# Expert-choice routing in a fused attention and MoE kernel: the chosen tokens by place and gather instead of a product over all tokens

## The chip, the cores and the metric

The kernel runs on one core of a Trainium2 chip. The metric is the device time of one execution in microseconds (us), the median of several runs. Names of engines: PE is TensorE (matmul), PEld its weight load, DVE VectorE, ACT ScalarE, POOL GpSimd, SP SyncE, which here issues nearly all DMAs. All data is fp32.

## The reference, cut to what matters

The input is four images x[B=4, C=128, 64, 64]; S = 4096 places of an image are its tokens. Layer 0 is group norm, three 1x1 convolutions with PReLU, and a softmax attention over all places with 64-wide queries and keys. Layer 1 is, on tokens, a layer norm with an attention of width 128, then a layer norm with a mixture of 64 experts in which each expert chooses tokens:

```python
logits = einsum('bsd,ed->bse', x, gate_w) + gate_b
probs = softmax(logits, axis=1)                      # over the tokens
vals, idx = top_k(probs.transpose(0, 2, 1), 8)       # 8 tokens per expert
gathered = take_along_axis(x, idx)                   # [b, 8, 64, 128]
pooled = einsum('bked,bke->bed', gathered, topv)
h = gelu([pooled, 1] @ weight1[e])                   # 128(+1) -> 512
out = [h, 1] @ weight2[e]                            # 512(+1) -> 128
outputs = zeros; outputs.at[idx].add(out * topv)     # scatter-add, then residual
```

## The kernel before, in words

The work is cut into 8 query blocks of 512 tokens per image and layer; a block goes through 8 groups of four 128-key chunks. A step of the main loop is one group: scores on PE (L526), exp on ACT (L535), and one step later the product with the values on PE (L460 for layer 0, L488 for layer 1). In layer 0 DVE sums the exps (L547, L550); in layer 1 DVE forms sums and differences of the values' and exps' halves (L474 to L476, the "mix") for a product with fewer multiplications.

Eight attentions follow each other as `stage(image, layer, beside, ...)`: (0,0), (1,0), (0,1), (2,0), (1,1), (3,0), (2,1), (3,1). In each step a stage advances, by one item, a generator `beside` (norms, convolutions, keys, routing), one for the next block's queries, and the finishing work of the block before, `after`; a barrier of the scheduler ends the step, so the order of each engine's instructions is nearly that of the program. The engines work their own queues in order and wait for each other by semaphores; buffers come from pools by tag, and a new tile in a tag waits for the last reader of what lay there.

The finish of a layer-1 block (`finish_attn`) norms the tokens (L174 is the norm's power, on POOL; L175 to L178 and L333 on DVE), stores the normed tokens `tb` to DRAM (L627 or L639), and leaves logits in M (a pair of images shares a tile, experts of one on each 64 partitions) with the eight largest of each 512 as candidates (L665). The last block's residual tokens in channels are `xp`, stored by L630.

The routing of image b, `route(b, take)`, goes: the eight largest logits of each expert (L689); a copy z of the logits in which these eight are replaced by a large negative value (L692, match_replace over 64x4096); exp of M with its sum (L700); exp of z (L710); the difference M = exp(M) - exp(z), which holds the eight weights at their places and zeros elsewhere (L711; on POOL for b = 0 to 2, on DVE for b = 3). Then the tokens are loaded (L678, eight of 256 KB), M is transposed by 32 PE transposes (L737, copied by ACT at L740), and 64 matmuls (as the profile counts them; L729) give the pooled tokens of the experts in two halves, which are scaled by the inverse sums (`inv2`, L718 to L722; L747) and added by a small matmul against `twin` (L750, L751). M stays for the scatter at the end: a product of the experts' outputs with M.

Routing 0 runs beside the stage (2,0), routing 1 beside (3,0), routing 2 beside (3,1), and routing 3 in the tail after all attention. The tail: `w1b` and seven token blocks are loaded, then weights 2 to 5 into a ring of four buffers (weights 0 and 1 are there already); the last block is finished; routing 3; weights 6, 7, 8 into buffers named k, z and v, 9 to 15 through the ring (L830, L834; 2.1 MB for each group of four experts). The FFN runs over 16 groups: first product (L912, `ph`), transposes (L922), GELU, second product (L942, `po`). Then the y tiles are read back (L976), the scatter product (L989) is added to them (L994) and they are stored from ACT's queue (L996).

The kernel takes its exps without subtracting a maximum. A guard therefore checks sums and inverses (L1466 to L1480, thirteen small DVE instructions), adds the verdicts over the partitions with a matmul (L1486, `pc`), reads the `count` (L1487) and branches: if a check fails, a general version runs, which with these inputs it doesn't.

Of the kernel before, what the change touches and what calls it, by code (L numbers as in the profile page):

```python
# [9 lines left out]
F32 = mybir.dt.float32  # L10
AF = mybir.ActivationFunctionType
ALU = mybir.AluOpType
# [14 lines left out]
def tile_unshifted(  # L27
# [48 lines left out]
    def ms_tile(name):  # L76
        return ps_ms.tile([P, BLK], F32, tag="ms", name=name)

    def block_tile(tag, name, bufs=2):
        pool = pools[of_pool.get(tag, "blk")]  # L80
        return pool.tile([P, BLK], F32, tag=tag, name=name, bufs=bufs)

    def dram_tile(shape, name):
        return dram.tile(shape, F32, tag=name, name=name)
# [5 lines left out]
    t1 = [[dram_tile([P, BLK], f"t1_{b}_{n}") for n in range(NB)] for b in range(B)]  # L90
    t2 = [[dram_tile([P, BLK], f"t2_{b}_{n}") for n in range(NB)] for b in range(B)]
    x1T = [[dram_tile([P, SUB, C], f"xT_{b}_{n}") for n in range(NB)] for b in range(B)]
    tokens = [[dram_tile([P, SUB, C], f"tk_{b}_{n}") for n in range(NB)] for b in range(B)]
    first_pair = dram_tile([P, S], "first_pair")

    e1 = [[dram_tile([CR, BLK], f"e1_{b}_{n}") for n in range(NB)] for b in range(B)]
# [463 lines left out]
    def finish_conv(b, n):  # L560
# [18 lines left out]
        yield  # L579
        turn_to_tokens(xp, block_tile("tb", f"xt{nm}"), x1T[b][n])  # L580

    def finish_attn(b, n):
        nm = f"{b}_1_{n}"
        av = avs.pop((b, 1, n))
# [39 lines left out]
        tg = block_tile("c1", f"tg{nm}")  # L624
        if b == B - 1 and n == NB - 1:
            norm_tokens(xT, tb, f"l2_{b}_{n}")
            nc.sync.dma_start(out=tokens[b][n], in_=tb)  # L627
            xp = block_tile("xp", f"xp{nm}")
            to_channels(xT, xp, f"x2_{b}_{n}")
            nc.sync.dma_start(out=x2[b][n], in_=xp)  # L630
            yield
            to_channels(tb, tg, f"l2_{b}_{n}")
        else:
            turn_to_channels(
                xT.rearrange("p s c -> p (s c)"), block_tile("xp", f"xt{nm}"), x2[b][n]
            )
            yield
            norm_tokens(xT, tb, f"l2_{b}_{n}")
            nc.sync.dma_start(out=tokens[b][n], in_=tb)  # L639
            turn_to_channels(  # L640
                tb.rearrange("p s c -> p (s c)"), block_tile("c0", f"tt{nm}"), t2[b][n]
            )
            yield
            yield
            nc.sync.dma_start(out=tg, in_=t2[b][n])
            yield
# [22 lines left out]
    pooled = keep.tile([P, E, B], F32, tag="pooled", name="pooled")  # L669


    twin = const.tile([P, 2, E], F32, tag="twin", name="twin")
    for h in range(2):
        nc.gpsimd.tensor_add(twin[:, h, :], ident[:, :E], ident[:, E:])
    inv_tot = keep.tile([P, B // 2], F32, tag="inv_tot", name="inv_tot")

    def load_tokens(b, tok, n):
        nc.sync.dma_start(out=tok[:, bass.ts(n, SUB), :], in_=tokens[b][n])  # L678

    def route(b, take):  # L680

        hs = slice((b % 2) * E, (b % 2 + 1) * E)
        m = M[b // 2][hs, :]
        neg = small.tile([P, 1], F32, tag="r_neg", name=f"r_neg{b}")
        tot = small.tile([P, 4], F32, tag="r_tot", name=f"r_tot{b}")
        top = small.tile([P, 8], F32, tag="r_top", name=f"r_top{b}")
        nc.vector.max(out=top[hs, :], in_=cand[b][hs].rearrange("p n k -> p (n k)"))  # L689
        nc.vector.tensor_scalar(neg[hs, :], top[hs, 0:1], -1.0, None, op0=ALU.mult)  # L690
        z = take("z")[hs, :]
        nc.vector.match_replace(  # L692
            out=z, in_to_replace=top[hs, :], in_values=m, imm_value=-3.0e38
        )
        yield
        own = take("e")
        ex = m if own is None else own[hs, :]
        quarter = [bass.ts(i, S // 4) for i in range(4)]
        for i, part in enumerate(quarter):
            nc.scalar.activation(  # L700
                ex[:, part], m[:, part], AF.Exp, bias=neg[hs, :], accum_out=tot[hs, i : i + 1]
            )
            if i % 2 == 1:
                yield
        inv = inv_tot[hs, b // 2 : b // 2 + 1]
        nc.vector.tensor_reduce(tot[hs, 0:1], tot[hs, :], axis=AX.X, op=ALU.add)
        nc.vector.reciprocal(inv, tot[hs, 0:1])
        subtract = nc.vector.tensor_sub if b == B - 1 else nc.gpsimd.tensor_sub
        for i, part in enumerate(quarter):
            nc.scalar.activation(z[:, part], z[:, part], AF.Exp, bias=neg[hs, :])  # L710
            subtract(m[:, part], ex[:, part], z[:, part])  # L711
            if i % 2 == 1:
                yield
        tok = take("tok")
        for n in range(NB - 1 if b == B - 1 else 0, NB):
            load_tokens(b, tok, n)
        p2 = ms_tile(f"inv2_{b}")
        nc.tensor.matmul(  # L718
            p2[:, 0:1], lhsT=twin[hs].rearrange("p h e -> p (h e)"), rhs=inv, start=True, stop=True
        )  # L720
        inv2 = small.tile([P, 1], F32, tag="r_inv2", name=f"inv2_{b}")
        nc.vector.tensor_copy(inv2, p2[:, 0:1])  # L722
        mT = take("mT")
        per = BLK // E

        def pool_tokens(pp, js):

            for j in js:
                nc.tensor.matmul(  # L729
                    pp[bass.ts(j % 2, E), :C], lhsT=mT[:, j, :], rhs=tok[:, j, :],  # L730
                    start=(j < 2), stop=(j >= NJ - 2),
                )

        for g in range(NJ // per):
            pm = ms_tile(f"pmt{b}_{g}")
            for s in range(per):
                nc.tensor.transpose(  # L737
                    pm[:, bass.ts(s, E)], m[:, bass.ts(g * per + s, P)], ident[hs, hs]
                )
            nc.scalar.copy(mT[:, bass.ts(g, per), :], pm.rearrange("p (s e) -> p s e", e=E))  # L740
            yield
        pp = ms_tile(f"pp{b}")
        pool_tokens(pp, range(NJ))
        if b == 1:
            nc.sync.dma_start(out=first_pair, in_=M[0])
        halves = take("halves")[:, :C]
        nc.vector.tensor_scalar(halves, pp[:, :C], inv2, None, op0=ALU.mult)  # L747
        yield
        pq = ms_tile(f"pool{b}")
        nc.tensor.matmul(pq[:, :E], lhsT=halves, rhs=twin[:, 0, :], start=True, stop=True)  # L750
        nc.vector.tensor_copy(pooled[:, :, b], pq[:, :E])  # L751
        yield


    def run(gen):
# [55 lines left out]
    def take_from_seq(b):  # L811
        def take(what):
            if what == "e":
                return None
            if what == "halves":
                return block_tile("c0", f"{what}{b}")
            shape, tag = {
                "z": ([P, S], "k"), "tok": ([P, NJ, C], "k"), "mT": ([P, NJ, E], "v")
            }[what]
            return seq.tile(shape, F32, tag=tag, name=f"{what}{b}")  # L820
        return take


# [36 lines left out]
    ring = ctx.enter_context(tc.tile_pool(name="ring", bufs=4, side="right", reuse_waits="tile"))  # L860
    w1b = seq.tile([E, H], F32, tag="mixed", name="w1b", bufs=1)
    nc.sync.dma_start(out=w1b, in_=a["weight1"][:, D1 - 1, :])
    last_tok = seq.tile([P, NJ, C], F32, tag="v", name=f"tok{B - 1}")
    for n in range(NB - 1):
        load_tokens(B - 1, last_tok, n)
    for g in range(2, 6):
        weights(g, ring, "w")
    while after:
        step_after()
    ends["blk"].close()  # L870
# [11 lines left out]
    nc.gpsimd.memset(pooledT, 0.0)  # L882

    def take_late(what):
        if what == "tok":
            return last_tok
        shape, pool, tag = {
            "z": ([P, S], late, "z"), "e": ([P, S], seq, "k"), "mT": ([P, NJ, E], seq, "mixed"),
            "halves": ([P, H], late, "hp"),
        }[what]  # L890
        return pool.tile(
            shape, F32, tag=tag, name=f"{what}{B - 1}", bufs=2 if tag in ("k", "v", "hp") else 1
        )

    run(route(B - 1, take_late))
    nc.vector.tensor_copy(pooledT[:, :, 0:B], pooled)

    weights(6, seq, "k")
    weights(7, late, "z")
    weights(8, seq, "v")  # L900
    for g in range(9, E // EG):
        weights(g, ring, "w")
    outT = late.tile([P, B, E], F32, tag="outT", name="outT")
# [542 lines left out]
def tile_conv_attn_hybrid(ctx: ExitStack, tc: tile.TileContext, a: dict, out: bass.AP):  # L1446
# [15 lines left out]
    nc.gpsimd.memset(top_inv, 0.0)  # L1462
    tile_unshifted(tc, a, out, all_sum, all_inv, top_sum, top_inv)

    ok = guard.tile([P, 4], F32, tag="ok", name="ok")
    nc.vector.tensor_reduce(ok[:, 0:1], all_sum, axis=AX.X, op=ALU.max)  # L1466
    nc.vector.tensor_reduce(ok[:, 1:2], all_inv, axis=AX.X, op=ALU.max)
    nc.vector.tensor_scalar(ok[:, 0:1], ok[:, 0:1], SAFE_SUM, None, op0=ALU.is_le)
    nc.vector.tensor_scalar(ok[:, 1:2], ok[:, 1:2], SAFE_INV, None, op0=ALU.is_le)
    nc.vector.tensor_reduce(ok[:, 2:3], top_sum, axis=AX.X, op=ALU.max)  # L1470
    nc.vector.tensor_reduce(ok[:, 3:4], top_inv, axis=AX.X, op=ALU.max)
    nc.vector.tensor_mul(ok[:, 2:3], ok[:, 2:3], ok[:, 3:4])
    nc.vector.tensor_scalar(ok[:, 2:3], ok[:, 2:3], SAFE_RATIO, None, op0=ALU.is_le)

    nc.vector.tensor_reduce(ok[:, 3:4], top_inv, axis=AX.X, op=ALU.add)
    nc.vector.tensor_scalar(ok[:, 3:4], ok[:, 3:4], SAFE_INV, None, op0=ALU.is_le)
    both = guard.tile([P, 1], F32, tag="both", name="both")
    nc.vector.tensor_mul(both, ok[:, 0:1], ok[:, 1:2])
# [52 lines left out]
```

## Time and profile before

| what | value |
|---|---|
| median of 3 runs | 3380.47 us (3379.44 to 3382.62) |
| the profiled execution | 3380.46 us, span 3378.6 us |
| busy PE / DVE / ACT / POOL | 97% / 64% / 37% / 12% of the span |
| exp L535 | x1024, 1024 ns each |
| transposes L737, products L729 | 12.5 us and 17.3 us in sum over four routings |
| match_replace L692 | x4, 4406 ns (median) |
| difference L711 | POOL x12, mean 2929 ns; DVE x4, mean 1223 ns |
| the page's DMA rate in the last two of 40 slices | 251 and 355 GB/s |

Spans and starts are counted from the first instruction of the profiled execution. A group of instructions has one line of the kernel, an engine, its operands, a count, a busy sum, the mean of one and the idle time of the engine ahead of it with what ended that. "SPq" is SP's queue, on which DMAs are issued. A chain of waits is followed back from the last instruction: at each step to what released it or to the instruction before it on its engine. Matmuls that follow each other overlap, so their durations add up to more than the time they take.

### The profile page before, as it was taken

How to read it: one execution, taken by the hardware profiler on the slowest of the kernel's cores; microseconds unless marked ns; L12 is line 12 of the kernel's file. 1: busy time of each engine (PE TensorE's matmuls, PEld its weight loads, DVE VectorE, ACT ScalarE, POOL GpSimd, SP SyncE). 2: the span in 40 equal slices, each digit the busy share in tenths (PEclk: the TensorE clock that was granted, in tenths of full speed). 3: DMA queues.
4: the chain of work that ended last, by engine and by line, in shares of the span. 5: the costliest groups of instructions: out<-in, count | busy, mean ns of one | idle time of the engine just before them, and what ended most of it. 6: DMA issues, size and time to landing. Idle time of an engine off the chain costs nothing.

```text
span 3378.6 us, 49187 instructions
## 1 busy us (share of the span) xinstructions
PE 3289.2 (97%) x19784; PEld 1576.0 (47%) x19784; DVE 2158.6 (64%) x4152; ACT 1252.7 (37%) x1429; POOL 415.4 (12%) x394
## 2 busy tenths in 40 slices
PE   7999999999999999999999999999999999999966
PEld 4444444444444545444444445444454545454442
DVE  6675577556675666766766566775775656665643
ACT  3333333333333353333333344333333333433330
POOL 0111123310000012250000002242000001100000
PEclk9999999999999999999999999999999999999977
DMA  3121122001120112211210112220321101120169
GB/s 91 39 47 26 41 50 64 18 29 44 35 45 19 35 26 60 66 26 29 47 36 20 32 35 72 51 53 19 66 48 26 32 17 32 41 76 23 26 251 355
DMA packets 351165, 181.52 MB, mean 54 GB/s; under 512 B 275536, under 2 KB 284624, under 8 KB 350672
## 3 DMA queue, kind: packets, MB, share of 16 engines
q1 hardware_dynamic: 344256, 168.36, 19.2%
q10 hardware_dynamic: 6672, 9.93, 0.8%
q8 instruction: 157, 2.57, 0.3%
q14 instruction: 80, 0.66, 0.1%
HBM read 117.54 MB, written 56.23 MB: 51 GB/s over the span
## 4 chain that ended last, share of the span: by engine, by line
PE 93%; DVE 2%; issue 2%; DMA 1%; ACT 0%; SPq 0%; POOL 0%; ACTq 0%; DVEq 0%; POOLq 0%
PE ps L526 38%; PE av L460 26%; PE av L488 22%; PE pe L264 1%; PE pa L280 1%; PE pd L572 1%; PE pq L429 1%; PE pv L608 1%; DMA out_dram<-y 1%; PE po L942 1%; PE ph L912 1%; PE pp L729 1%; DMA w<-in_weight_dram 0%; PE pg L657 0%; DVE tt L474 0%
## 5 line engine op out<-in xcount | busy, mean ns | idle before, releaser
L535 ACT ACTIVATE pt<-ps 128x1024 f32<-128x1024 f32 x1024 | 1021.0, 1024 | 1556.9 <-PE ps L526 1465.3
L526 PE MATMUL ps<-q,t 128*64 128x512 f32 x4096 | 927.5, 594 | 0.0
L460 PE MATMUL av<-pt,asm 64*128 64x512 f32 x4096 | 923.1, 589 | 0.9 <-ACT sw L591 0.9
L550 DVE TENSOR_TENSOR sacc<-sacc,pt 128x1024 f32<-128x1024 f32 x448 | 569.6, 1271 | 206.0 <-ACT pt L535 177.5
L488 PE MATMUL av<-pt,tt 128*64 128x256 f32 x3072 | 637.4, 379 | 0.0
L460 PEld LDWEIGHTS av<-pt,asm 64*128 64x128 f32 x4096 | 404.0, 187 | 477.2 <-issue 461.8
L474 DVE TENSOR_TENSOR tt<-pt 128x512 f32<-128x512 f32 x512 | 356.9, 697 | 381.5 <-ACT pt L535 363.0
L488 PE MATMUL av<-tt,mixed 128*64 128x256 f32 x2048 | 526.5, 380 | 0.4 <-DVE tt L474 0.4
L526 PEld LDWEIGHTS ps<-q,t 128*64 128x64 f32 x4096 | 290.2, 137 | 497.2 <-issue 462.2
L526 PE MATMUL ps<-e,e 64*128 64x512 f32 x2048 | 491.1, 597 | 0.0
L488 PEld LDWEIGHTS av<-pt,tt 128*64 128x64 f32 x3072 | 354.1, 137 | 292.1 <-issue 143.4
L488 PE MATMUL av<-tt,tt 128*64 128x256 f32 x1024 | 305.3, 380 | 4.6 <-DVE tt L476 4.6
L488 PE MATMUL av<-pt,mixed 128*64 128x256 f32 x1024 | 305.1, 380 | 1.4 <-DVE pt L475 1.4
L526 PEld LDWEIGHTS ps<-e,e 64*128 64x128 f32 x2048 | 194.6, 187 | 235.1 <-issue 231.5
L174 POOL TENSOR_TENSOR l_y<-l_v,mhalf 128x4 f32<-128x4 f32 x64 | 64.6, 1009 | 1774.8 <-DVE l_v L173 1774.5
L488 PEld LDWEIGHTS av<-tt,mixed 128*64 128x64 f32 x2048 | 280.9, 137 | 3.0 <-DVE tt L474 0.9
L476 DVE TENSOR_TENSOR tt<-pt 128x256 f32<-128x256 f32 x512 | 220.0, 430 | 16.6
L475 DVE TENSOR_TENSOR pt<-tt,pt 128x256 f32<-128x256 f32 x512 | 218.9, 428 | 16.4
L488 PEld LDWEIGHTS av<-pt,mixed 128*64 128x64 f32 x1024 | 140.4, 137 | 74.9 <-DVE pt L475 1.9
L488 PEld LDWEIGHTS av<-tt,tt 128*64 128x64 f32 x1024 | 140.5, 137 | 6.0 <-DVE tt L476 5.0
L574 DVE RECIPROCAL inv<-pd 128x512 f32<-128x512 f32 x32 | 107.4, 3357 | 33.7 <-PE pd L572 33.7
L569 POOL TENSOR_TENSOR all_sum<-all_sum,c 128x512 f32<-128x512 f32 x32 | 42.0, 1314 | 548.4 <-DVE c L568 537.1
(188 smaller groups left out, 1819.6 us busy)
## 6 DMA issues: line engine op xcount, KB each, us to landing
w<-in_weight_dram SPq DMA_DIRECT2D x32, 1024.0 KB, 12.0
xq<-in_x_dram SPq DMA_DIRECT2D x32, 256.0 KB, 3.5
xT<-xt SPq DMA_DIRECT2D x128, 64.0 KB, 2.2
ak<-xT SPq DMA_DIRECT2D x32, 256.0 KB, 3.2
t<-kt SPq DMA_DIRECT2D x128, 64.0 KB, 2.2
t<-t SPq DMA_DIRECT2D x32, 256.0 KB, 3.1
xr<-xT SPq DMA_DIRECT2D x32, 256.0 KB, 2.9
tk<-tb SPq DMA_DIRECT2D x32, 256.0 KB, 2.0
```

Source lines behind the costliest of these rows:

```text
L174: nc.gpsimd.tensor_tensor(y[:, :k], v[:, :k], mhalf[:, :k], op=ALU.pow)
L264: nc.tensor.matmul(pe, lhsT=w12, rhs=xn, start=True, stop=True)
L460: nc.tensor.matmul(avs[b, 0, n][:, r, :], lhsT=values[b, 0][rows, j, :], rhs=pt[rows, h, :], start=(j == 0), stop=(j == NJ - 1),)
L474: nc.vector.tensor_sub(tt[:, 0:2, :], p4[:, :, 1, :], p4[:, 0, :, :])
L475: nc.vector.tensor_add(p4[:, 0, 1, :], tt[:, 1, :], p4[:, 0, 0, :])
L476: nc.vector.tensor_sub(tt[:, 2, :], p4[:, 1, 0, :], p4[:, 0, 1, :])
L488: nc.tensor.matmul(av[bass.ts(half, HC), bank, slot, :], lhsT=lhsT, rhs=rhs, start=first, stop=final, skip_group_check=True,)
L526: nc.tensor.matmul(ps[part, h, :], lhsT=key[:, part], rhs=q[rows, :], start=True, stop=True,)
L535: nc.scalar.activation(pt, ps, AF.Exp, scale=scale)
L550: nc.vector.tensor_add(sums[b, n], sums[b, n], pt)
L569: nc.gpsimd.tensor_add(all_sum, all_sum, c1)
L574: nc.vector.reciprocal(r, pd)
```

## The change

The routing finds the places of the eight largest logits (max_index) instead of making a weighted sum over all 4096 tokens. The tokens are stored as rows of a [4096, 128] array in DRAM; the first four places of each expert go to partitions 0 to 63, the other four to 64 to 127, and four indirect DMAs on POOL's queue fetch 128 rows of 512 bytes each. The eight weights are exps of the eight logits times the inverse sum; one tensor_scalar and three multiply-adds on DVE give `halves`, which the small matmul adds as before. The difference M is still made for the scatter, now after the pooled tokens; the match_replace follows one step later (b < 3) or behind the weights (b = 3). Token loads, transposes, mT, inv2 and products go. In the tail, the seven token loads go, weights 6 are issued right behind weights 5, and 7 and 8 change their buffers. The last block's token store is issued by ACT. The guard's reductions are kept in program order, behind the rest of the kernel.

```diff
-    tokens = [[dram_tile([P, SUB, C], f"tk_{b}_{n}") for n in range(NB)] for b in range(B)]
+    tokens = [dram_tile([S, C], f"tk_{b}") for b in range(B)]
...
+    def store_tokens(b, n, tb):
+        rows = tokens[b][bass.ts(n, BLK), :].rearrange("(s p) c -> p s c", p=P)
+
+        q = nc.scalar if b == B - 1 and n == NB - 1 else nc.sync
+        q.dma_start(out=rows, in_=tb)
...
-            nc.sync.dma_start(out=tokens[b][n], in_=tb)
+            store_tokens(b, n, tb)
...
-    twin = const.tile([P, 2, E], F32, tag="twin", name="twin")
-    for h in range(2):
-        nc.gpsimd.tensor_add(twin[:, h, :], ident[:, :E], ident[:, E:])
+    twin = const.tile([P, E], F32, tag="twin", name="twin")
+    nc.gpsimd.tensor_add(twin, ident[:, :E], ident[:, E:])
...
+    KH = 4
     def route(b, take):
...
         nc.vector.max(out=top[hs, :], in_=cand[b][hs].rearrange("p n k -> p (n k)"))
         nc.vector.tensor_scalar(neg[hs, :], top[hs, 0:1], -1.0, None, op0=ALU.mult)
-        z = take("z")[hs, :]
-        nc.vector.match_replace(
-            out=z, in_to_replace=top[hs, :], in_values=m, imm_value=-3.0e38
-        )
+        nc.vector.max_index(out=at[hs, :], in_max=top[hs, :], in_values=m)
         yield
         own = take("e")
-        ex = m if own is None else own[hs, :]
+        if own is None:
+            ex, z = m, take("z")[hs, :]
+            nc.vector.match_replace(
+                out=z, in_to_replace=top[hs, :], in_values=m, imm_value=-3.0e38
+            )
+        else:
+            ex = own[hs, :]
+        got = take("got")
+        for h in range(2):
+            nc.vector.tensor_copy(rows[h * E : (h + 1) * E, :], at[hs, bass.ts(h, KH)])
+        for k in range(KH):
+            nc.gpsimd.indirect_dma_start(
+                out=got[:, bass.ts(k, C)], out_offset=None, in_=tokens[b],
+                in_offset=bass.IndirectOffsetOnAxis(ap=rows[:, k : k + 1], axis=0),
+            )
+        yield
         quarter = [bass.ts(i, S // 4) for i in range(4)]
...
+        w8 = small.tile([P, 8], F32, tag="r_w8", name=f"r_w8{b}")
+        nc.scalar.activation(w8[hs, :], top[hs, :], AF.Exp, bias=neg[hs, :])
         inv = inv_tot[hs, b // 2 : b // 2 + 1]
         nc.vector.tensor_reduce(tot[hs, 0:1], tot[hs, :], axis=AX.X, op=ALU.add)
         nc.vector.reciprocal(inv, tot[hs, 0:1])
+        for h in range(2):
+            nc.vector.tensor_scalar(
+                wgt[h * E : (h + 1) * E, :], w8[hs, bass.ts(h, KH)], inv, None, op0=ALU.mult
+            )
+        if own is not None:
+            z = take("z")[hs, :]
+            nc.vector.match_replace(
+                out=z, in_to_replace=top[hs, :], in_values=m, imm_value=-3.0e38
+            )
+        halves = take("halves")[:, :C]
+        nc.vector.tensor_scalar(halves, got[:, :C], wgt[:, 0:1], None, op0=ALU.mult)
+        for k in range(1, KH):
+            nc.vector.scalar_tensor_tensor(
+                halves, in0=got[:, bass.ts(k, C)], scalar=wgt[:, k : k + 1], in1=halves,
+                op0=ALU.mult, op1=ALU.add,
+            )
+        yield
+        pq = ms_tile(f"pool{b}")
+        nc.tensor.matmul(pq[:, :E], lhsT=halves, rhs=twin, start=True, stop=True)
+        nc.vector.tensor_copy(pooled[:, :, b], pq[:, :E])
         subtract = nc.vector.tensor_sub if b == B - 1 else nc.gpsimd.tensor_sub
...
-        tok = take("tok")
...
-        for g in range(NJ // per):
-            pm = ms_tile(f"pmt{b}_{g}")
-            for s in range(per):
-                nc.tensor.transpose(
-                    pm[:, bass.ts(s, E)], m[:, bass.ts(g * per + s, P)], ident[hs, hs]
-                )
-            nc.scalar.copy(mT[:, bass.ts(g, per), :], pm.rearrange("p (s e) -> p s e", e=E))
-            yield
-        pp = ms_tile(f"pp{b}")
-        pool_tokens(pp, range(NJ))
...
-    last_tok = seq.tile([P, NJ, C], F32, tag="v", name=f"tok{B - 1}")
-    for n in range(NB - 1):
-        load_tokens(B - 1, last_tok, n)
     for g in range(2, 6):
         weights(g, ring, "w")
+    weights(6, seq, "v")
...
-            "z": ([P, S], late, "z"), "e": ([P, S], seq, "k"), "mT": ([P, NJ, E], seq, "mixed"),
-            "halves": ([P, H], late, "hp"),
+            "z": ([P, S], late, "z"), "e": ([P, S], seq, "k"),
+            "got": ([P, KH * C], late, "hp"), "halves": ([P, H], late, "hp"),
...
-    weights(6, seq, "k")
-    weights(7, late, "z")
-    weights(8, seq, "v")
+    weights(7, seq, "k")
+    weights(8, late, "z")
...
+    later = tc.keep_in_program_order
-    nc.vector.tensor_reduce(ok[:, 0:1], all_sum, axis=AX.X, op=ALU.max)
-    nc.vector.tensor_reduce(ok[:, 1:2], all_inv, axis=AX.X, op=ALU.max)
+    later(nc.vector.tensor_reduce(ok[:, 0:1], all_sum, axis=AX.X, op=ALU.max))
+    later(nc.vector.tensor_reduce(ok[:, 1:2], all_inv, axis=AX.X, op=ALU.max))
...
```

## The prediction

> **What bounds the kernel now.** I read the page first: the busy table, the granted clock, the chain that ended last.
>
> ```profile
> PE 3289.2 (97%) x19784; PEld 1576.0 (47%) x19784; DVE 2158.6 (64%) x4152; ACT 1252.7 (37%) x1429; POOL 415.4 (12%) x394
> PEclk9999999999999999999999999999999999999977
> PE 93%; DVE 2%; issue 2%; DMA 1%; ACT 0%; SPq 0%; POOL 0%; ACTq 0%; DVEq 0%; POOLq 0%
> ```
>
> TensorE (PE) is busy 97% and is 93% of the chain, at full clock in 38 of 40 slices. The last two slices are different: clock 0.7, DMA 251 and 355 GB/s against a mean of 54. So there are two stages: a bulk (to 3227 us) in which each microsecond of PE work removed is a microsecond gained if nothing else gets in front of PE, and a tail in which transfers set the pace. The change touches both.
>
> In the bulk, what does one routing cost on PE? The chain of waits over the first routing answers:
>
> ```profile
> 1273.27 3.43 PE av L460 x16
> 1276.70 0.11 PE inv L718
> 1276.81 0.49 PE pmt L737 x7
> 1277.30 1.83 PE ps L526 x8
> 1279.13 3.43 PE av L460 x16
> 1282.57 0.43 PE pmt L737 x7
> ...
> 1300.87 3.65 PE pp L729 x64
> 1304.51 1.92 PE ps L526 x8
> ```
>
> An ordinary step is scores 1.72 plus products 3.43 = 5.15 us; the pieces of the routing stand between them with no gap: they are on the path.
>
> The third routing (b=2) runs beside a token layer, and there PE waits, by its list of waits near 2920 us and the timeline:
>
> ```profile
> PE av L488 <- DVE tt L476: 4.6, 1, 4.6
> PE av L488 <- DVE pt L475: 1.4, 1, 1.4
> 2913.68 10.36 POOL L711 TENSOR_TENSOR M<-M,z 64x1024 f32<-64x1024 f32 x4 [2.47 <-ACT z L710]
> 2913.83 2.77 DVE L474 TENSOR_TENSOR tt<-pt 128x512 f32<-128x512 f32 x1
> ```
>
> The mix on DVE, 0.70 us by its mean, takes 2.77 beside POOL's subtract. With the pipeline refilling, that step takes some 15.5 us (2911.75 to about 2927) against 6.46 for a usual one: about 9 us lost.
>
> In the tail, the chain and SP's waits:
>
> ```profile
> 3252.09 4.43 DVE z L692
> 3263.58 6.18 PE pp L729 x64
> 3271.48 1.92 PE ph L912 x16
> SPq L830 <- PE po L942: 18.5, 4, 11.9
> SPq L678 <- DMA tk<-tb: 9.0, 1, 9.0
> SPq L830 <- DVE M L711: 3.2, 1, 3.2
> ```
>
> The first FFN product starts at 3271.48 after match_replace, exp, subtract, transposes and the 64 products. Weights 9 and on wait for the FFN to give buffers back (11.9 us, group 2's product): from there the transfers, and with them the end, follow the FFN's start. So the tail's question is when ph starts and how fast the first groups run, not how much the routing computes.
>
> [...] the granted clock is 0.50 from 3235 to 3265 and 1.00 in 3275 to 3285, after work from 3259 on. [...] So I price max_index as a match_replace, 4.4 us; the trace has no max_index.
>
> **Part 1: PE work removed, three routings in the bulk.** Transposes 0.49+0.43+0.43+0.58 = 1.93, inverse 0.11, scores slowed behind them (1.83 for 1.72, three times) 0.3, products pp 3.65: 6.0 us. The one pool matmul stays. Three times: **-18.0**. The 24 token loads of 256 KB and the copies to mT also go; they were hidden beside PE (DMA mean share 0.1 to 0.2) and give nothing.
>
> **Part 2: work added in the bulk.** Per routing: DVE one max_index 4.4, halves as one tensor_scalar and three multiply-adds (about 0.35 each by L747's 0.348) 1.4 instead of 0.35, and five small ones of 0.15; ACT one tiny exp; POOL four gathers. DVE is 64% busy, so as a sum it fits; what counts is who queues behind it. The exp of M works in place, so it now waits for a match_replace that stands one step later behind max_index; on ACT, in order, the exps of the scores (L535) stand behind it. For b=0 and 1 I put that exp near 1258.8; the exp of group 3 behind it then ends some 1 to 2 us after PE wants its buffer for the next scores. Cost 1.5 each, bounds 0 and 3: **+3.0**.
>
> For b=2 the mix of DVE, which PE waits for, is queued behind max_index and match_replace: by the order of instructions one mix comes about 2.7 us late. Then the token norm's pow (L174, POOL, 1.01 us) stands behind the four gathers, DVE waits for it, PE for the mix. How long does a gather hold POOL? Nothing in the trace shows it. At least 0.1 us (POOL's smallest instruction); [...] four hold it 4.4, and with a slack of 0.4 there PE waits about 4. The four subtracts remain and still collide with the mix, now when DVE is less behind: 0 to 2. Sum 7.7 against 9 lost now: I take **0** for the difference, bounds -4 and +4.
>
> **Part 3: the tail.** The seven token loads (1.84 MB) go, and the loads of weights 6 (2.1 MB) take their place ahead of the last stores, so the queue up to the x2 store is as long as before: that store, issued at 3249.24 and landing 10.2 us later (3259.4), lands at about 3260. The match_replace of b=3 writes a new buffer z; laying out the buffers by their sizes, z now lies over xp, the source of that store, because got is allocated ahead of it. So match_replace, with its buffer free at 3252.09 before, waits for the landing: 3260.4. Then 4.4 (to 3264.8), exp 1.14, four subtracts at 1.22 with exps beside them, four halves 1.4 and two copies of 0.27 and 0.31 among them: pooledT at about 3272.0, ph at **3272.1 against 3271.48, +0.6**. Removed (pmt 2.13, pp 6.18) and added nearly cancel. The gathers wait for the last token store and land by about 3260, behind match_replace: nothing.
>
> But PE now has no work between about 3244 and 3272, where transposes and products warmed it from 3259. It starts the FFN at half clock; [...] **+2.5** (1.7 to 3.5). Weights 7 wait for the last subtract, so they are issued near 3271.7 (weights 6 and 7 before: 3262.38 and 3263.42) and the DMA queues idle longer; but weights 9 wait for the FFN as before, 7 and 8 land by 3284 and are wanted after 3290. No cost as such. Tail: **+3.1**, bounds -10 (the x2 wait does not bind, ph 8 us earlier, 1.84 MB less, at 390 GB/s 4.7 us) and +6.
>
> **Part 4: the guard's checks.** Thirteen small DVE instructions move from 3226-3240, beside the last products, to behind the last add. Five of them took 3226.26 to 3227.93 = 1.67; the other eight at 0.12 to 0.2 from start to start are 1.3. The end follows them: last add until 3371.24, pc 3371.30, count 3371.52, branch 3372.5, 5.2 us of branch, span's end 3378.6. The cover was the last products; now there is none: **+3.0** (2.5 to 3.5). At 3226 nothing is gained: DVE is not the bound there.
>
> **Sum:** -18.0 + 3.0 + 0 + 3.1 + 3.0 = **-8.9**. The profiled execution took 3380.46 us (span 3378.6, 1.9 around it), the median of the runs shown is 3380.47: they agree, so no correction. 3380.5 - 8.9 = 3371.6.
>
> **Rivals.** A, the sum above, 3371.6, chance 0.50. B, the tail gains too: the x2 store lands before the DVE gets there, or z's wait is for something early. For it: nothing in the trace shows this buffer's wait, it is my reading of the layout. Against it: the store lands 10.2 us after issue behind 10 MB of weights. Then the tail is about -8 for +3.1: 3360.5, chance 0.15. C, the bulk's gain is mostly eaten: PE leaves its slot, but the ACT and DVE queues, each with max_index and match_replace ahead of PE's food, let PE wait 3 us in each of b=0 and 1 and 4 more in b=2, which with the ends' costs gives about 3379, within 0.2% of before: chance 0.25. D, slower: the gathers hold POOL. In b=2 each further microsecond per gather delays the pow, and so PE, by 4. From 1.1+8.9/4 = 3.3 us per gather the gain is gone; from 5.0 us the kernel is slower by over 0.2%; at 6 us: 3371.6 + 4 x 4.9 = 3391. [...] Chance 0.10. That the change does not do what it says: the 64 products and 32 transposes per routing do vanish from the instruction streams, so I give that nothing.
>
> **Numbers.** 0.2% is 6.8 us, about what a measurement of this kernel can tell. Faster by more: A mostly (3363 to 3376, of which 0.08 falls within 0.2%), B: 0.60. Same: C and A's edge: 0.29. Slower: D and C's far edge: 0.11. The range 3358 to 3384 holds A, most of B and C, and leaves out D.
>
> **What would show it.** Right: the steps of the chain in the first routing are 5.15 us without gaps; no L729 or L737 rows; PE's waits near 2920 again sum to 6 to 9 us; match_replace of b=3 released by the x2 store; ph at 3272 minus the bulk's 15, at clock 0.5; the checks between the last add and pc. Wrong: PE waits over 2 us in routings 0 and 1 (C), DVE waiting for POOL over 6 us (D), ph over 5 us earlier relative to the last product (B), checks taking other than 3 us.

## The result, and the profile after

The changed kernel takes 3369.29 us (median; 3367.72 to 3370.07) against 3381.38 for the kernel before on the same chip: ratio 0.9964, 95% interval 0.9947 to 0.9981. It is faster by 12 us; the two profiled spans differ by 11.3 (3378.6 and 3367.3).

The page of the changed kernel: the busy table, the granted clock and the new DMA queue.

```profile
PE 3261.8 (97%) x19392; PEld 1539.9 (46%) x19392; DVE 2179.4 (65%) x4184; ACT 1244.3 (37%) x1417; POOL 432.2 (13%) x409
PEclk9999999999999999999999999999999999999977
q0 software_dynamic: 512, 1.05, 0.1%
```

PE has 27 us less work and 392 matmuls fewer. The q0 row (packets, MB, share) is new: the sixteen gathers, 1.05 MB. PE is still the bound of the bulk.

The same place as in the first chain shown, PE in the timeline beside routing 0 (start, duration, instruction):

```profile
1273.78 3.60 PE L460 MATMUL av<-pt,asm 64*128 64x512 f32 x16
1277.31 0.43 PE L748 MATMUL pool<-twin,halves 128*128 128x64 f32 x2
1277.67 1.99 PE L526 MATMUL ps<-e,e 64*128 64x512 f32 x8
1279.49 3.60 PE L460 MATMUL av<-pt,asm 64*128 64x512 f32 x16
1282.92 1.45 PE L526 MATMUL ps<-e,e 64*128 64x512 f32 x6
```

Of the routing only the pool matmul is left on PE; the next step goes from 1277.67 to 1282.92 without transposes. PE's waits near routing 2, DVE's and ACT's waits around it, in the changed kernel:

```profile
PE av L488 <- DVE tt L474: 5.2, 2, 3.9
DVE l_z L175 <- POOL l_y L174: 4.8, 1, 4.8
ACT M L720 <- DVE z L704: 6.8, 1, 6.8
```

The columns are the sum, the number and the longest. PE's stall on L475 and L476 has gone: beside POOL's subtract they had taken 2.47 and 2.56 us (at 2916.63 and 2921.77 before), and now take 0.42 and 0.43 (at 2914.20 and 2914.65). A stall of similar length has come: DVE waits 4.8 us for the norm's power. The tail, in the chain of waits:

```profile
3231.30 13.10 DMA x<-xp
3244.66 4.41 DVE z L736
3256.30 3.64 PE ph L909 x16
3355.82 1.22 DVE y L991
3357.04 0.59 DVE ok L1465
```

Match_replace of the last routing is released by the landing of the x2 store, ph starts with a slow first stretch (3.64 us for 16 records, 1.92 before; granted clock 0.50), and behind the last add stand the checks.

Where the 11.3 us come from is read by comparing the two traces exp by exp (the 1024 exps of L535 are the same in both) and by marks in the tail:

| place | predicted | trace |
|---|---|---|
| routing 0 | -4.5 | -5.0 |
| routing 1 | -4.5 | -4.3 |
| routing 2: the stall | 0 | -0.1 |
| routing 2: PE work behind it | -6.0 | -8.3 |
| start-up and two short stalls elsewhere | 0 | +1.2 |
| last product to first ph (43.93, now 45.24) | +0.6 | +1.3 |
| first ph to last add (99.76, now 100.74) | +2.5 | +1.0 |
| last add to end (7.34, now 10.21) | +3.0 | +2.9 |
| sum | -8.9 | -11.3 |

The two rows of routing 2 are split at the first exp behind the stall (2929.58 before, 2921.35 after): up to it both kernels had lost the same. The row after them is not the change's. The first exp came at 27.3 us before and at 28.5 in the changed kernel; over the profiled executions of this study, in kernels whose start is the same, it differs by up to 1.3 us. And one stretch of 3.41 us at half clock falls at 811 us before and at 1677 us in the changed kernel. Each costs 1.6 us and is no stall, since PE works in it; before:

```profile
811.00:814.50 3.50, 3.50 (x11) 1.08 (x12) 1.80 (x3) 0.69 (x1) 0.00 (x0) 0.51 0.03 5
```

The columns are start and end, length, busy PE, PEld, DVE, ACT and POOL (with the number of instructions), then the granted clock, the DMA queues' busy share and GB/s.

### The profile page after: what moved, and what is told of

It is laid out like the page before. It is cut to its first block, busy times and chain, and to the rows that moved or that the text cites. A ratio compares the mean times of both kernels' runs of the same rounds, so it can differ in the third digit from the quotient of the medians.

```text
span 3367.3 us, 48432 instructions
## 1 busy us (share of the span) xinstructions
PE 3261.8 (97%) x19392; PEld 1539.9 (46%) x19392; DVE 2179.4 (65%) x4184; ACT 1244.3 (37%) x1417; POOL 432.2 (13%) x409
## 3 DMA queue, kind: packets, MB, share of 16 engines
q0 software_dynamic: 512, 1.05, 0.1%
## 5 line engine op out<-in xcount | busy, mean ns | idle before, releaser
L535 ACT ACTIVATE pt<-ps 128x1024 f32<-128x1024 f32 x1024 | 1020.8, 1024 | 1566.3 <-PE ps L526 1475.3
L460 PEld LDWEIGHTS av<-pt,asm 64*128 64x128 f32 x4096 | 396.1, 187 | 485.0 <-issue 470.5
L476 DVE TENSOR_TENSOR tt<-pt 128x256 f32<-128x256 f32 x512 | 221.8, 433 | 16.5
L475 DVE TENSOR_TENSOR pt<-tt,pt 128x256 f32<-128x256 f32 x512 | 218.6, 427 | 16.3
```

What stands on the lines that cost most here:

```text
L460: nc.tensor.matmul(avs[b, 0, n][:, r, :], lhsT=values[b, 0][rows, j, :], rhs=pt[rows, h, :], start=(j == 0), stop=(j == NJ - 1),)
L475: nc.vector.tensor_add(p4[:, 0, 1, :], tt[:, 1, :], p4[:, 0, 0, :])
L476: nc.vector.tensor_sub(tt[:, 2, :], p4[:, 1, 0, :], p4[:, 0, 1, :])
L535: nc.scalar.activation(pt, ps, AF.Exp, scale=scale)
```

## The experiments

Each starts from the kernel before or from the changed kernel ("after"). Times per routing are again differences of the L535 exps.

**1. The PE work alone: e7_before_no_products.** Before, with

```diff
         for g in range(NJ // per):
+            if own is None:
+                yield
+                continue
             pm = ms_tile(f"pmt{b}_{g}")
...
-        pool_tokens(pp, range(NJ))
+        if own is not None:
+            pool_tokens(pp, range(NJ))
+        else:
+            for j in range(2):
+                nc.tensor.matmul(
+                    pp[bass.ts(j, E), :C], lhsT=tok[:, j, :E], rhs=tok[:, j, :],
+                    start=True, stop=True,
+                )
```

> The kernel before, without the 32 transposes, their copies and the 64 products in routings 0 to 2 (two small products take their place; the pooled tokens of three images are not those of the reference). All else stays: token loads, match_replace in its old step, POOL's subtracts. Theory (in the bulk PE's own work is the path): 5.8 to 6.1 us less in each routing, 17 to 18.5 in all, about 3363.5; the stall of some 9 us at routing 2 stays. Rival (without these PE pieces other engines come to bind, since they gave DVE and ACT time to catch up): under 4 us per routing, and new PE waits for DVE or ACT of 2 us or more in routings 0 and 1.

Measured 3362.86 us, ratio to before 0.9947 (0.993 to 0.9964). Routings 0 and 1 took 5.37 us less each, routing 2 took 6.96 less: 17.7 in sum, as expected, though none of the three lies within 5.8 to 6.1. PE's waits in the stall of routing 2 are those of before to the tenth (4.6, 1.4, 0.4 us). So removed PE work is gained nearly whole; the rival falls. A fourth wait, 40 us behind that stall, stands in the list of before and is gone here:

```profile
PE pmt L737 <- DVE xT L617: 1.3, 1, 1.3
```

Routing 2's transposes waited there for DVE's finishing work on the block before (L617), so removing them gave more than their own length. Behind the stall routing 2 gained 7.57 us here; 0.6 of that was lost at the stall itself, where the half clock (experiment 3) lay 1.2 us later against the work than in before. The experiment also shows that this removal without gathers, second search and late checks gives more than the whole change.

**2. The exps in place: e5_exp_late.** After, with one more `yield` behind the gathers.

> The changed kernel, with one more step between the gathers and the exps of the logits. Theory (in routings 0 and 1 the exps of M, in place, wait 4.9 us for match_replace, and the exps of the scores stand behind them on ACT, which costs PE 1.2 and 1.9 us): ACT's wait for match_replace disappears, group 3's exp is on time, routings 0 and 1 give 1.2 and 1.9 us back, routing 2 is unchanged within 1 us: about 3366.2. Rival (the stall comes from the sums on DVE, which queue behind match_replace and release the exps' buffers late): the stall of 1.2 and 1.9 us stays where it is.

Routing 0 gained 1.14, routing 1 gained 1.88, routing 2 gained 0.77; 3363.21 us, ratio to before 0.9948 (0.9931 to 0.9964). The expected 3366.2 lies within that interval. The 0.77 is not the edit's: e3 (experiment 6), which leaves the bulk as it is, has the same 0.77 there, and experiment 3 tells from what. ACT's wait for match_replace fell from 17.3 us in three waits to 0.4, and PE's wait for the exps, 2.4 us in after, is gone. In after's timeline of ACT the mechanism stands in two lines:

```profile
1258.27 1.15 ACT L720 ACTIVATE M<-M,r_neg 64x1024 f32<-64x1024 f32 x1 [4.94 <-DVE z L704]
1260.56 1.91 ACT L535 ACTIVATE pt<-ps 128x1024 f32<-128x1024 f32 x2
```

ACT sat idle for 4.94 us with an instruction that could not start, and the scores' exp came behind it.

**3. The gathers on POOL: e4_gather_late.** After, with the gathers moved one step on:

```diff
+        yield
         for k in range(KH):
             nc.gpsimd.indirect_dma_start(...)
-        yield
```

> The changed kernel, with only the four gathers moved one step later (the exps stay in their step). Theory (in routing 2 the norm's power on POOL stood 4.8 us behind the gathers, and PE's longest wait of 3.9 us came from that): DVE's wait for the power falls from 4.8 to about 1.2 us, PE's wait for the mix from 5.2 to under 2 us, routing 2 costs 3 to 4 us less, routings 0 and 1 are unchanged: about 3365.7. Rival (the mix is late because max_index and match_replace stand ahead of it, and POOL's delay lies in their shadow): PE's wait stays above 4 us and the time within 1 us of 3369.3.

Measured 3362.72 us, ratio to before 0.9949 (0.9932 to 0.9966); routing 2 gained 5.94 us, routings 0 and 1 nothing (0.00). PE's wait for the mix fell from 5.2 to 1.5, which is 3.7; 2.2 more came from somewhere. POOL in after, timeline:

```profile
2905.03 1.05 POOL L713 DMA_INDIRECT got<-tk,r_rows  x1 [60.26 <-DVE r_rows L711]
2906.39 0.95 POOL L713 DMA_INDIRECT got<-tk,r_rows  x1 [0.31 <-issue]
2907.64 0.94 POOL L713 DMA_INDIRECT got<-tk,r_rows  x1 [0.30 <-issue]
2908.89 0.94 POOL L713 DMA_INDIRECT got<-tk,r_rows  x1 [0.30 <-issue]
2909.84 1.06 POOL L174 TENSOR_TENSOR l_y<-l_v,mhalf 128x4 f32<-128x4 f32 x1
```

A gather holds POOL 0.95 us and the next starts 1.25 after it; the power waits for all four. The rest is the clock. Windows of after near the stall (columns as in the window above):

```profile
2909.00:2914.00 5.00, 1.28 (x9) 0.42 (x5) 2.90 (x10) 2.30 (x5) 1.88 (x2) 0.85 0.14 37
2914.00:2919.00 5.00, 4.78 (x23) 2.69 (x25) 4.79 (x12) 0.00 (x0) 0.00 (x0) 0.50 0.50 101
```

PE idled 3.93 us, and the clock was 0.50 for the next 5: 23 matmuls in that window, where e4's windows at the same times hold 33 and 40 at clock 1.00. By the clock record of the trace it was at half from 2912.53 to 2919.36. For 5.1 us of that PE was at work again, and half of 5.1 is about the missing 2.2.

In the clock records of before and after the clock changes only on a grid of 3.41 us. In the bulk (60 to 3190 us) it fell to half four times, each time behind a piece of this grid in which PE had idled for 2.02 to 2.25 us (from 807.69 and 2917.13 before, from 1673.49 and 2909.12 in after); behind the pieces at full clock in which PE idled 1.68 us or less it stayed full. No sharp limit shows: in after's tail it fell behind 1.78 us of idle time (from 3301.65) and stayed full behind 1.84 (from 3209.49). So what a stall cost here depended on how it lay on the grid. In e3 the same stall of 3.9 us was followed by 3.41 us of half clock instead of 6.83, and routing 2 took 0.77 us less.

**4. Twice the gathers: e8_double_gather.** After, with four more gathers into a spare buffer in routings 0 to 2.

> The changed kernel, with four further gathers (into a buffer that is never read) behind the four of routings 0 to 2. Each holds POOL 1.25 us from start to start. Theory: in routings 0 and 1 POOL has nothing that PE waits for, so they cost under 0.5 us each; in routing 2 the norm's power comes 5 us later and PE waits 4.5 to 5 us more: about 3374. Rival (the queue behind the power has slack): under 2 us in all, 3369 to 3371. [...]

3373.87 us, ratio to before 0.9981 (0.9974 to 0.9988). Routings 0 and 1 cost 0.01 us each; routing 2 cost 3.96 more, DVE's wait for the power went from 4.8 to 9.8 and PE's longest from 3.9 to 8.9. The wait grew by the predicted 5.0, the time by 1.0 less. The half clock again lasted 6.83 us (2914.87 to 2921.70), but PE came back at 2918.70, so that only 3.0 us of it were worked through, against 5.1 in after; half of the 2.1 between them is 1.1.

```profile
2919.00:2924.00 5.00, 5.00 (x29) 2.53 (x27) 4.79 (x13) 0.00 (x0) 0.00 (x0) 0.73 0.52 93
```

So the place of the gathers in POOL's queue, ahead of the norm's power, decides: in routings 0 and 1 the same four cost 0.01 us.

**5. The checks: e1_before_guard_last and e2_after_guard_early.** `later` on the five reductions of before; in after, `later = lambda made: made`.

> The kernel before, with only the five reductions of the guard kept in program order, so that all thirteen checks stand behind the last add. Theory (part 4 of the sum, the checks have no cover at the end): from the end of the last add to the end of the count 3.2 us instead of 0.43, span longer by 2.8 us, 3383 to 3385 us; nothing gained near 3226, where the last products end at the same time within 0.3 us. Rival (the checks' removal from the last block's DVE work starts the tail earlier by the 1.7 us that five of them took there): ph starts 1.7 us earlier after the last product and the time stays within 1.2 us of before.

> The changed kernel, with the guard's checks placed by the scheduler as in the kernel before. Theory: the last add and all before it as in the changed kernel within 0.5 us, count 2.8 us earlier after the last add, about 3366.5 us. Rival (the early place costs the tail, since the last block's DVE chain is now on the path to the routing): the tail starts 1.7 to 3 us later and the gain is under 1 us.

From the last add to the count it is 0.43 us with the checks early and 3.24 with them late, in both kernels: 2.8. In e1 the last product and ph stand as in before within 0.3 us, so the rival of an earlier tail falls; in e2 ph came 0.8 us later after the last product, more than the 0.5 expected. The whole time moved by less. e1 is at 3381.91 us, ratio 1.0006 (0.9998 to 1.0015), not distinguishable from before; in its trace the last add to the end took 1.9 us more, and ph to the last add 1.5 less, which hides it. e2 is at 3366.82, ratio 0.9958 (0.9944 to 0.9973), which these runs don't tell from after's 0.9964. From the count to the end it took 6.97 us in after, but 8.47 in e2 and 10.88 in the combined kernel below, both with early checks. The place of the checks is not what makes that long, since e3, e6, e9 and e10 have late checks and took 8.16 to 9.13. A late last store goes with it: its last packet ended 0.6 to 1.2 us after the count in five kernels (0.6 in after), whose end came 6.0 to 8.0 after the count, and 4.0 to 8.0 after the count in six others, whose end came 8.2 to 10.9 after it; in before it ended 3.6 after the count, and the end came 6.9 after it. So the checks may have a partial cover, the last stores' landing; how much of the 2.8 it takes was not settled.

**6. The x2 wait: e3_z_clear.** After, with

```diff
-            "got": ([P, KH * C], late, "hp"),
+            "got": ([P, KH * C], seq, "mixed"),
```

> The changed kernel, with only the place of one buffer changed: got of the last routing lies in the tag mixed (free since w1b was transposed), so that z no longer lies over xp; halves then does. Theory (the match_replace waited 9.6 us for the landing of the last x2 store): it starts at about 3235 instead of 3244.6, its wait moves to the halves, which wait for the same landing at about 3244.4 but have only the subtracts behind them, so ph starts near 3251.5 instead of 3256.3, 4 to 5 us earlier; as weights 7 to 9 follow, the end moves by 4 to 5 us, to about 3364.5. Rival 1 (the transfers set the tail whatever the start of the FFN): ph is earlier, but the end moves by less than 1 us. Rival 2 (the gathers' landing is the wait behind it): the halves wait for the gathers until 3245 or later, and ph gains under 3 us.

DVE's waits for DMA in the tail, first line after, second line e3:

```profile
DVE z L736 <- DMA x<-xp: 9.6, 1, 9.6
```

```profile
DVE halves L740 <- DMA x<-xp: 8.5, 1, 8.5
```

Match_replace started 22.6 us after the last product instead of 33.6, and the wait passed to the halves, as expected; ph came 2.8 us earlier (42.45 after the last product), not 4 to 5: the same landing came 2 us later after the last product here (the halves started at 35.5, match_replace in after at 33.6), and the subtracts still lay ahead of pooledT. The time, 3360.68 us (ratio 0.9939, 0.9923 to 0.9956), fell by 8.6: more than ph. Of the 7.9 between the profiled spans, 1.7 lie ahead of the tail, where the edit changes nothing (0.9 at the start, 0.8 by the clock), 2.8 are ph's and 5.3 lie between ph and the last add (95.40 instead of 100.74); behind the last add 1.9 were lost. The trace shows a possible reason for the 5.3: the scheduler, with other lengths ahead of it, had moved the 2 MB reload of M (M0b) ahead of weights 9, into the time in which SP waits for the FFN's second group.

**7. That load alone: e9_m0b_early.** After, with the two lines of M0b moved behind `weights(8, ...)`.

> The changed kernel, with one DMA moved: the reload of the first pair's M (2 MB) is issued ahead of weights 9 instead of behind weights 15. Question: two kernels with another tail gained 5 us more than their start of the FFN did, and in both the scheduler had moved this load there. Theory (the load fills a hole in which the queues wait for the FFN's group 2, and the stream behind it is one load shorter): ph as in the changed kernel, from ph to the last add 95.4 instead of 100.7 us, so about 3364. Rival (those gains came from the FFN's start, and the load only delays weights 9): 3369 or more.

3367.39 us, ratio to before 0.9963 (0.9949 to 0.9977): the whole time does not tell it from after (0.9964). In the trace ph to the last add took 97.79 us, 2.95 less, and the last add to the end 1.2 more. Right in kind, half in size: a new hole came at 3330 to 3340, where the queues were busy 65%. So of e3's 5.3 us from ph to the last add some 3 are this load's; the rest goes with it in a way that was not taken apart.

**8. The cold start: e6_warm.** After, with eight products of got that nobody reads, five ahead of the pool matmul and three behind it.

> The changed kernel, with eight idle products of 128x512 on PE (their result is never read) in the last routing, five before and three after the pool matmul, reading got. Theory (the FFN starts at half clock because PE had nothing to do): the granted clock is near 1.0 when ph starts, the first 16 records of ph take 1.9 us instead of 3.64, weights 9 are issued 2 us earlier relative to ph, and the end moves by 1 to 2 us, to about 3368. Rival (the cold start is made up again later, since the FFN waits for transfers after group 9): the first groups are faster but the end stays within 0.5 us of 3369.3.

The first 16 records of ph took 2.05 us instead of 3.64, and weights 9 came 11.44 us after ph instead of 13.28, as before the change (11.29). So the half clock (0.50 from 3256 to 3260 in after, 0.80 in e6) costs 1.8 us there. The products delayed ph by 0.8. The time, 3364.32 us (ratio 0.9951, 0.9935 to 0.9968), is not evidence for it: here, too, the scheduler moved M0b forward.

**9. A tail without these waits, and all together: e10_tail and e11_all.** e10 is after with got in "mixed", halves in a small buffer of its own, and the last routing's exps and subtracts (`differences`) ahead of the halves; here, too, M0b is moved forward:

```diff
+        if own is not None:
+            yield from differences()
         halves = take("halves")[:, :C]
-        nc.vector.tensor_scalar(halves, got[:, :C], wgt[:, 0:1], None, op0=ALU.mult)
+        made = nc.vector.tensor_scalar(halves, got[:, :C], wgt[:, 0:1], None, op0=ALU.mult)
+        if own is not None:
+            tc.keep_in_program_order(made)
```

> The changed kernel with another tail: got in the tag mixed, halves of the last routing in a small buffer of its own, and the last routing's exps and subtracts ahead of the halves, so that nothing in it waits for the x2 store; the scheduler moves the reload of M ahead of weights 9 here, too. Theory (three serial costs: the x2 wait, the hole of 11 us in which no transfer runs until weights 7 find a buffer, and the reload at the end): match_replace at once after the weights of the eight, the subtracts end 31 us after the last product, weights 7 follow without a hole, ph 36 to 37 us after the last product instead of 45.2, bounded by the gathers' landing; the last add 11 to 13 us earlier, about 3357. Rival (the transfers were bound anyway, the hole is only moved): under 9 us.

3355.96 us, ratio to before 0.9928 (0.9911 to 0.9944). The subtracts ended 33 us after the last product, ph came after 36.09, weights 7 were issued at 3244.20 instead of 3255.86, and the last add came 14.5 us earlier, a little over the 11 to 13; the whole time fell by 13.3. Windows of after and of e10 at the same times, after first (last two columns: busy share of the DMA queues, GB/s):

```profile
3240.00:3250.00 10.00, 0.00 (x0) 0.00 (x0) 5.32 (x5) 0.90 (x1) 0.00 (x0) 0.50 0.29 106
3250.00:3260.00 10.00, 4.35 (x19) 1.31 (x20) 6.57 (x9) 4.63 (x5) 0.00 (x0) 0.50 0.28 94
```

```profile
3240.00:3250.00 10.00, 3.35 (x18) 1.19 (x18) 6.77 (x11) 3.89 (x4) 0.40 (x1) 0.50 0.80 266
3250.00:3260.00 10.00, 10.00 (x147) 5.63 (x143) 5.49 (x8) 1.90 (x4) 0.00 (x0) 0.97 1.04 370
```

In after nothing at all is moved from 3245 to 3255 (share 0.00 over these 10 us); in e10 most of that hole is closed. The three edits and the moved load were not told apart here.

> All that gained, together: the tail of the kernel above, the guard's checks where the scheduler puts them, the gathers one step later and the exps one more step later, and the reload of M ahead of weights 9. Theory (the parts lie at different places and add): guard -2.5, routings 0 and 1 -3.0, routing 2 -6 to -7, tail -12: about 3345. Rival (the two moves in routing 2 collide, since exps and POOL's subtracts come later, into the next block's work): routing 2 gains under 4, 3348 to 3351.

e11 adds the early checks, the early M0b and both moves of gathers and exps. 3344.51 us (3344.16 to 3345.87), ratio to before 0.9894 (0.9878 to 0.9911): 36 us faster than before, 25 faster than after. Routing 0 gained 1.14, routing 1 gained 1.88, routing 2 gained 5.93, each what its experiment had given alone; e5's 0.77 in routing 2 does not come on top, since no half clock is left there. The two moves do not collide.

## Why the prediction was right

The direction, the size (-8.9 against -12.1, range 3358 to 3384) and nearly all mechanisms held. The size is in part luck: the two largest misses, PE work in routing 2 and the cold start, made the gain 3.8 us larger than forecast, while the start of the program, which is not the change's, and the later ph took 1.9 back. By its steps:

- **Part 1** (-18.0). Outside their stalls routings 0 and 1 became 6.16 and 6.15 us shorter, where the chain's pieces had given 6.0: that PE's pieces lay on the path with no gap held there. In routing 2 the work behind the stall became 8.3 shorter. The sum took routing 0's chain for all three and left out the wait of 1.3 us ahead of routing 2's transposes (experiment 1); the last 0.8 beyond 6.2 was not taken apart.
- **Part 2, routings 0 and 1** (+1.5 each). Taking the wait away gave 1.14 and 1.88. The step that carried it was to ask which queue the waiting exp stands in.
- **Part 2, gathers.** The hold of 1.1 us per gather was a guess of the author's: no trace before shows a gather. It is 1.25 from start to start in after, DVE's wait 4.8, PE's 3.9 (predicted about 4). Max_index, which no trace before shows either, was priced as a match_replace, 4.4 us, and took 4.416.
- **Part 2, routing 2** (difference 0, bounds -4 and +4). It was -0.1, by luck more than by the sum, which added up waits and left the clock out, though part 3 priced a half clock. PE's waits fell from 6.4 to 5.2 us (the sign named for being right, 6 to 9, did not come). But of the 6.83 us of half clock, which both kernels have there, PE worked through 3.0 before and through 5.1 after, and half of the 2.1 between them took the gain back.
- **Part 3.** The x2 wait is shown, in the chain and by e3; ph at +1.3 instead of +0.6. The cold start's 2.5 was the author's estimate: ph started at 3256.30 and the clock was at half until 3260.69, and it cost 2.0 at weights 9 and only 1.0 at the last add. "No cost as such" for the late weights 7 fits, since nothing beyond the cold start appeared, but it hid that this hole was what the tail had to give.
- **Part 4** (+3.0). 2.8 to the count. That the end follows the count is only part of it, as experiment 5 shows.
- **Rivals.** C (the bulk's gain eaten) did not come: the waits were as in the sum. D's price was right in kind: each gather's 1.25 us reaches PE, experiment 4; its duration was not. B's ground, that the x2 wait does not bind, was wrong; what B promised is what e10 then built.

## What to carry to other kernels

When an engine's own work is removed from the path, look at the queues that the new work is put in: here one instruction that waits in ACT's queue cost 1.1 to 1.9 us, and four gathers ahead of a 1 us power cost 5.9, and a moved or added `yield` took each away. A stall of PE can cost a slow stretch after it as well: here 2.02 to 2.25 us of idle time within 3.41 us were each followed by half clock. So a gain or loss of 1 to 2 us in one trace may be the clock's and not the edit's (one stretch of 3.41 us cost 1.6); look at the granted clock before you explain it. In a stage that transfers bound, compare the holes in the DMA's busy share, not the compute: a buffer laid over another's source, the order of subtracts and halves, and a load issued after the last weights were together worth 14.5 us at the last add, not far from the 18 that was forecast for the routings' PE work.

## What the runs showed of the hardware that was not expected

- An indirect DMA of 128 rows of 512 bytes held POOL 0.94 to 2.01 us (median 0.947, 16 of them in after), the first of a group 1.03 to 2.01, with 0.30 us between two; the last of each group landed 2.5 to 5.5 us after its start.
- In the bulk of before and after the clock fell to half four times, each time behind a piece of a 3.41 us grid in which PE idled 2.02 to 2.25 us, and stayed there for one piece or two. A stall of 3.93 us (after) so cost some 6 us, and one of 8.95 us (e8) only 4.0 more than that.
- The end of the program came 6.0 us after the count in e1, 6.97 in after, 8.0 in e8 and 10.88 in e11, with the same code there.
